# Layer 2 of a four-layer convolution kernel: PSUM tiles handed out in turn under names of their own

## The chip, the cores and the metric

One core of one Trainium2 chip runs one program. The metric is the device time of an execution in microseconds (us). Engines: PE is TensorE (its weight loads are listed as PEld), DVE is VectorE, ACT is ScalarE, POOL is GpSimd, SP is SyncE, which here issues the DMAs.

## The reference

An input of 32 images, 96 channels, 56 x 56, passes four layers, each of the form x = x + layer(groupnorm(x)), with 32 groups of three channels. Layer 0 is an inverted bottleneck with squeeze and excitation, layer 1 a wavelet convolution, layer 3 a depthwise 9 x 9 diffusion filter. The change is in layer 2, a quantised inverted bottleneck:

```python
h = bn(conv1x1(groupnorm(x), quant_w(w1)))      # 96 -> 576 channels
h = act_q(h)                                    # clip to 0..1, round to 4 bits
h = bn(depthwise3x3(h, quant_w(w2)))            # 576 channels
h = act_q(h)
h = bn(conv1x1(h, quant_w(w3)))                 # 576 -> 96
y = x_n + h                                     # x_n: the layer's normalised input
return x + y
```

## The kernel before

The layers run one after the other. Layer 2 (`layer2`, from 3620 to 5390 us of the profiled execution) goes over the 32 images. An image has 3136 positions, in eight row tiles of 392; the 576 channels are five blocks k = 0 to 4, the last with 64 channels. The work is cut into steps, written as a letter with indices in the string `L2_ORDER`, and `run_steps` plays this string once per pass n; a `-` after a step takes the image before n, a `+` the one after. PE, DVE and ACT execute exactly in the order in which the steps are recorded (`manual_schedule`), so one pass mixes three images:

- `e` (`expand`, L1107): for block k and quarter i of the image, four float32r matmuls (a high and a low part of the input, two row tiles) into one PSUM tile `ps`; then one eviction by `evict` into `u`, with scale, bias and rounding to int16. 20 of them per image.
- `m` (`activate`): DVE clips `u` into the padded bf16 image `apad`.
- `a` (`depthwise`, L1126): the 3 x 3 filter as matmuls of 64 x 64 diagonal matrices, four quadrants of the array at a time. For k < 4 and half h, 144 matmuls go into two PSUM tiles `psd`, for k = 4 72 in two steps with one tile each; 648 matmuls and 18 tiles per image. `evict` takes each tile to `a` or `a2c`. The eviction of half h, tile x of block k is called a{k}{h}{x} here.
- `n` (`activate2`): DVE clips it. `j` (`project`, L1163): ten matmuls into one tile `psj`, four times per image; `d` (`add`, L1170): DVE adds it to the image `xt`.
- `u`, `v` (L1045, L1053): tiny matmuls for the group norm, one PSUM tile each, read by DVE. `h` (`high`, L1079) on ACT and `l` (`low`, L1085) on DVE make the two parts of the next image's input. `s` and `o` take statistics (`channel_stats`); `o` also stores a finished pair of images and loads a later one (`store_images` L169, `fetch` L1016, by SP).

`evict` runs on ACT (L1097), but for four steps per image on DVE (L1095):

```python
L2_ON_DVE = {"e00", "e20", "a301", "a201"}
```

The depthwise steps of a pass come in this order, with what lies between them:

```python
a00 a10 o- a11 n1 a01 a20 h1+ a30 a21 l0+ a31 n0 a40 l1+ n2 l2+ a41 n3 n4
```

All PSUM tiles of layer 2 have the same shape, 128 x 2 x 512 float32 (two banks), and come from one pool of four under the tag "mm" (L1003). When a tile is asked for, the pool takes one of its four places; a tile that takes a place waits for the reads of the tile that had it before. An image takes 44 tiles: 18 `psd`, 20 `ps`, 4 `psj`, `pn` and `pv`. After the last pass `store_norm` (L95) takes one more.

Of the kernel before, what the change touches and what calls it, by code (L numbers as in the profile page):

```python
# [10 lines left out]
F32 = mybir.dt.float32  # L11
# [6 lines left out]
PSUM = bass.MemoryType.PSUM  # L18
# [73 lines left out]
    nc.vector.bn_aggr(mv, st.rearrange("c a b -> c (a b)"))  # L92


def store_norm(tc, S, pool, psum, mv, dram, bias, room=None):  # L95


    nc = tc.nc
    if room is None:
        room = pool.tile([C, 6 * B + 1], F32, tag="room", name="room", bufs=1)  # L100
    mc, d, dv, ve = (room[:C, i * B : (i + 1) * B] for i in range(4))
    row = room[:C, 4 * B : 6 * B + 1]
    rstd = row[:, 0:B]
    ps = psum.tile([128, 2, 512], F32, tag="mm", name="pn")
    nc.vector.tensor_copy(mc, mv[:, :, 0])
    nc.tensor.matmul(ps[:C, 0, :B], S.grp, mc, start=True, stop=True)
    nc.vector.tensor_tensor(d, mc, ps[:C, 0, :B], ALU.subtract)
    nc.vector.tensor_tensor(dv, d, d, ALU.mult)
    nc.vector.tensor_tensor(dv, dv, mv[:, :, 1], ALU.add)
    nc.vector.tensor_tensor(d, mc, d, ALU.subtract)  # L110
    nc.tensor.matmul(ps[:C, 1, :B], S.grp, dv, start=True, stop=True)
    nc.vector.tensor_scalar(ve, ps[:C, 1, :B], EPS_GN, None, ALU.add)
    nc.gpsimd.tensor_tensor(rstd, ve, S.mhalf[:C, :B], ALU.pow)
    nc.vector.scalar_tensor_tensor(row[:, B : 2 * B], d, -1.0, rstd, ALU.mult, ALU.mult)
    if bias is None:
        nc.vector.memset(row[:, 2 * B :], 0.0)
    else:
        nc.vector.tensor_copy(row[:, 2 * B :], bias)
    tc.keep_in_program_order(nc.sync.dma_start(dram, row))


def run_steps(step, image, order, done=""):

    for n in range(-2, B + 2):
        for s in order.split():
            b = n + s.count("+") - s.count("-")
            if 0 <= b < B and not (b == 0 and s.rstrip("+-") in done):
                step[s[0]](image(b), *map(int, s.rstrip("+-")[1:]))  # L130
# [53 lines left out]
def layer0(ctx, tc, S, x, w, y0, norm1, tables, aside):  # L184
# [363 lines left out]
    with tc.manual_schedule(engines=MANUAL):  # L548
        run_steps(step, image, L0_ORDER, FIRST)
    store_norm(tc, S, sm, psum, mv_all, norm1, S.bias1, hc.rearrange("p h w -> p (h w)"))  # L550


# [434 lines left out]
def layer2(ctx, tc, S, k2, y1, y2, norm3):  # L987
# [11 lines left out]
    pool = ctx.enter_context(tc.tile_pool(name="l2", bufs=1))  # L999
    sm = ctx.enter_context(tc.tile_pool(name="l2s", bufs=3))  # L1000
    up = ctx.enter_context(tc.tile_pool(name="l2u", bufs=3))
    ap = ctx.enter_context(tc.tile_pool(name="l2a", bufs=6))
    psum = ctx.enter_context(tc.tile_pool(name="l2p", bufs=4, space=PSUM))  # L1003
    CC, HALF, N9 = NBLK - 1, 64, 2 * NBLK - 1
    w1, w3, diag, s1, o1, s2, o2, s3, o3 = k2.constants

# [15 lines left out]

    apad = padded(cp, nc, NBLK, BF16, "apad")
    mv_all = cp.tile([C, B, 2], F32, tag="mv2", name="mv2")
    ims = {}

    def image(b):

# [5 lines left out]
    def small(name):  # L1034
        return sm.tile([C, 1], F32, tag=name, name=name)
# [5 lines left out]

    def group_mean(im):
        mean, var = im["mv"][:, 0:1], im["mv"][:, 1:2]
        ps = psum.tile([128, 2, 512], F32, tag="mm", name="pn")
        nc.tensor.matmul(ps[:C, 0, 0:1], S.grp, mean, start=True, stop=True)  # L1045
        gm, d, dv = (im.setdefault(n, small(n)) for n in ("gm", "d", "dv"))
        nc.vector.tensor_copy(gm, ps[:C, 0, 0:1])
        nc.vector.tensor_tensor(d, mean, gm, ALU.subtract)
        nc.vector.scalar_tensor_tensor(dv, d, d, var, ALU.mult, ALU.add)

    def group_variance(im):
        ps = psum.tile([128, 2, 512], F32, tag="mm", name="pv")
        nc.tensor.matmul(ps[:C, 0, 0:1], S.grp, im["dv"], start=True, stop=True)  # L1053
        ve = small("ve")
        nc.vector.tensor_scalar(ve, ps[:C, 0, 0:1], EPS_GN, None, ALU.add)
        im["rstd"] = small("rstd")
        nc.gpsimd.tensor_tensor(im["rstd"], ve, S.mhalf[:C, :1], ALU.pow)
# [34 lines left out]
    def evict(out, ps, s, o, c, on_dve):  # L1092

        if on_dve:
            nc.vector.tensor_scalar(out, ps, s[:, c : c + 1], o[:, c : c + 1], ALU.mult, ALU.add)  # L1095
        else:
            nc.scalar.activation(out, ps, AF.Identity, bias=o[:, c : c + 1], scale=s[:, c : c + 1])  # L1097

    def expand(im, k, i):

        if i == 0:
            im["u"][k] = up.tile([128, HW], I16, tag="u", name="u")
        ps = psum.tile([128, 2, 512], F32, tag="mm", name="ps")
        for j in range(2):
            r0 = (2 * i + j) * RT
            for part in ("hi", "lo"):
                nc.tensor.matmul(  # L1107
                    ps[:, j, :NT], w1[:, k * 128 : k * 128 + 128],
                    im[part][:, r0 : r0 + RT, :].rearrange("c h w -> c (h w)"),
                    start=(part == "hi"), stop=(part == "lo"),  # L1110
                )
        evict(im["u"][k][:, 2 * i * NT : 2 * (i + 1) * NT].rearrange("p (j n) -> p j n", j=2), ps[:, :, :NT],
              s1, o1, k if k < CC else N9 - 1, f"e{k}{i}" in L2_ON_DVE)
# [7 lines left out]
    def quarter(ps, k, t, r, c, j, tile):  # L1121

        p, q = (slice(x * HALF, (x + 1) * HALF) for x in (r, c))
        at = (tile * RT + t // 3) * PITCH + t % 3
        v = apad[k][p, at : at + RT * PITCH].rearrange("p (r w) -> p r w", w=PITCH)[:, :, 0:W]
        nc.tensor.matmul(ps[q, j, :NT].rearrange("p (r w) -> p r w", w=W), diag[p, k, t, :], v,  # L1126
                         start=(t == 0), stop=(t == 8))

    def depthwise(im, k, h):


        if h == 0:
            im["a2"][k] = (ap.tile([128, HW], BF16, tag="a2", name="a2") if k < CC else
                           ap.tile([128, HW // 2], BF16, tag="a2c", name="a2c", bufs=2))
        u = im["a2"][k].bitcast(I16)
        if k == CC:
            ps = psum.tile([128, 2, 512], F32, tag="mm", name="psd")
            for t in range(9):
                for c in range(2):
                    for j in range(2):  # L1140
                        quarter(ps, k, t, c ^ j, c, j, 4 * h + 2 * c + j)
            parts = [(h, ps, N9 - 1)]
        else:
            ps = [psum.tile([128, 2, 512], F32, tag="mm", name="psd") for _ in range(2)]
            for t in range(9):
                for j in range(2):
                    for x in range(2):
                        for r in range(2):
                            quarter(ps[x], k, t, r, r ^ x, j, 4 * h + 2 * x + j)
            parts = [(2 * h, ps[0], k), (2 * h + 1, ps[1], CC + k)]  # L1150
        for x, (n, p, c) in enumerate(parts):
            evict(u[:, 2 * n * NT : 2 * (n + 1) * NT].rearrange("p (m j x) -> p j m x", j=2, m=NPH),
                  p[:, :, :NT].rearrange("p j (x m) -> p j m x", m=NPH), s2, o2, c, f"a{k}{h}{x}" in L2_ON_DVE)
# [2 lines left out]
        clip(im["a2"][k], im["a2"][k].bitcast(I16))  # L1156

    def project(im, i):
        ps = im["ps"][i] = psum.tile([128, 2, 512], F32, tag="mm", name="psj")
        for j in range(2):  # L1160
            for k in range(NBLK):
                n, c = (2 * i + j, k + CC * (i % 2)) if k < CC else (2 * (i // 2) + j, N9 - 1 + i % 2)
                nc.tensor.matmul(ps[:C, j, :NT], w3[:, c, :], im["a2"][k][:, n * NT : (n + 1) * NT],  # L1163
                                 start=(k == 0), stop=(k == CC))
# [10 lines left out]
    def store(im):  # L1175
# [6 lines left out]

    step = {
        "s": stats, "u": group_mean, "v": group_variance, "b": residual_factors, "x": centre,
        "h": high, "l": low, "r": residual, "e": expand, "m": activate, "a": depthwise, "n": activate2,
        "j": project, "d": add, "o": store,
    }
    with tc.manual_schedule(engines=MANUAL):
        run_steps(step, image, L2_ORDER)
    store_norm(tc, S, sm, psum, mv_all, norm3, None)  # L1190


def diffusion_kernels(tc, cp, w, behind):
# [111 lines left out]
def kernel_body(tc, w, x, out):  # L1305
    nc = tc.nc
    with ExitStack() as ctx:
# [32 lines left out]
        with ExitStack() as ctx2:  # L1340
            k2 = Layer2(ctx2, tc, S, w, y1)

            def behind(pair):
                k2.prepare(pair)
                if not k2.stages:
                    k2.begin(min(2 * pair, C - GR))

            layer1(tc, w, y0, norm1, t1, t2, t3, y1, behind)
            k2.begin(C)
            layer2(tc, S, k2, y1, y2, norm3)  # L1350
# [143 lines left out]
```

## Time and profile before

| | |
|---|---|
| median of 3 runs | 5833.67 us (5833.61 to 5834.31) |
| profiled execution | 5845.79 us, span 5844.0 us |
| PE busy | 5504.4 us (94% of the span), 59688 matmuls |
| VectorE busy | 4693.6 us (80%) |
| ScalarE busy | 4182.6 us (72%) |
| depthwise matmuls of layer 2, L1126 | 935.9 us busy, 128.1 us idle before them |
| evictions of layer 2 on ScalarE, L1097 | 448 of `psd` to `a` (424.1 us), 576 of `ps` (536.9 us) |

A row of the page names line, engine, operation, and output<-inputs with shapes; then the number of instructions, their busy time and mean length in ns, and the idle time of the engine just before them with what ended it. "issue" stands for idle time that ended with no semaphore that the profile shows. A line of a timeline has start and length in us, engine, line, operation, how many were merged, and in brackets the idle time before it and its releaser. Times inside the span are counted from its start.

### The profile page before, as it was taken

The page shows a single profiled execution, that of the slowest core. Times are in us where ns is not written, and L with a number is a line of the kernel's source. Part 1 is how long each engine was busy: PE and PEld are TensorE (multiplying, and loading weights), DVE is VectorE, ACT ScalarE, POOL GpSimd, SP SyncE. Part 2 cuts the span into 40 slices and gives each one's busy share as a digit, 9 for nine tenths or more (in the row PEclk, how much of TensorE's full clock was granted, in tenths as well). Part 3 has the DMA queues.
Part 4 walks back from the last instruction along what each step waited for, and adds up shares of the span by engine and source line. Part 5 has one row for each costly group of instructions (what it writes and reads, how often), then busy time and mean ns, then how long its engine had stood idle before and what let it go on. Part 6 is the DMA issues. An engine that isn't in the chain of part 4 may idle for free.

```text
span 5844.0 us, 137224 instructions
## 1 busy us (share of the span) xinstructions
PE 5504.4 (94%) x59688; PEld 3074.4 (53%) x59688; DVE 4693.6 (80%) x5388; ACT 4182.6 (72%) x6036; POOL 240.1 (4%) x156
## 2 busy tenths in 40 slices
PE   5999999999999999995999997999899999897899
PEld 2333333333333333333566665777777777775444
DVE  6999999999999999994766665766667667665777
ACT  5888888888888888874565564766667677675555
POOL 5000000000000000000000000000000000000000
PEclk9999999999999999997999999999999999999999
DMA  3122333332222222235576668386796796754888
GB/s 98 18 56 56 62 60 57 58 58 54 56 49 48 55 52 56 46 26 89 144 141 147 154 147 89 26 44 42 49 46 37 51 49 40 50 31 34 234 253 245
DMA packets 1306412, 454.32 MB, mean 78 GB/s; under 512 B 1123841, under 2 KB 1301753, under 8 KB 1303889
## 3 DMA queue, kind: packets, MB, share of 16 engines
q1 hardware_dynamic: 1305809, 445.54, 50.3%
q8 instruction: 468, 7.67, 0.6%
q14 instruction: 135, 1.11, 0.1%
HBM read 284.44 MB, written 214.08 MB: 85 GB/s over the span
## 4 chain that ended last, share of the span: by engine, by line
PE 83%; ACT 6%; issue 4%; DVE 3%; DMA 2%; POOL 1%; SPq 1%; POOLq 0%; ACTq 0%; DVEq 0%
PE psd L432 17%; PE psd L1126 11%; PE psj L483 10%; PE ps L365 7%; PE pc L842 7%; PE ps L1107 7%; PE pse L388 6%; PE pc L1280 6%; PE psj L1163 3%; ACT hi L1079 2%; PE pc L826 2%; ACT a L1097 2%; PE pa L800 2%; PE pc L816 1%; ACT u L1097 1%
## 5 line engine op out<-in xcount | busy, mean ns | idle before, releaser
L406 DVE SCALAR_TENSOR_TENSOR h<-hpad,l_wdw,h 128x3136 f32<-128x3136 f32 x512 | 1782.2, 3481 | 9.1
L432 PE MATMUL psd<-plane,filt 128*32 128x392 f32 (+5 forms) x16384 | 1084.3, 485 | 0.0
L1126 PE MATMUL psd<-apad,diag 64*64 64x392 bf16 x20736 | 935.9, 333 | 128.1 <-issue 73.0
L1126 PEld LDWEIGHTS <-diag 64*64 64x64 bf16 x20736 | 705.0, 107 | 354.9 <-issue 184.8
L432 PEld LDWEIGHTS psd<-plane,filt 128*32 128x32 f32 (+1 forms) x16384 | 390.1, 108 | 675.2 <-issue 622.7
L1097 ACT ACTIVATE a<-psd,o,s 128x784 int16<-128x784 f32 x448 | 424.1, 999 | 347.8 <-PE psd L1126 347.7
L672 ACT COPY T<-raw 32x112 f32<-32x112 f32 (+2 forms) x1440 | 462.6, 384 | 267.6 <-DMA raw<-tdiff 219.9
L1097 ACT ACTIVATE u<-ps,o,s 128x784 int16<-128x784 f32 x576 | 536.9, 1003 | 160.2 <-PE ps L1107 141.8
L365 PE MATMUL ps<-xn,l_wboth 96*128 96x392 f32 (+1 forms) x1536 | 465.4, 505 | 23.9 <-ACT xn L347 23.0
L406 DVE SCALAR_TENSOR_TENSOR hc<-hhalf,l_wdw,hc 128x1568 f32<-128x1568 f32 x256 | 473.8, 1851 | 16.1 <-ACT hc L399 9.4
L1107 PE MATMUL ps<-hi,l_w1q 96*128 96x392 f32 x1280 | 461.7, 361 | 9.2 <-ACT hi L1079 9.2
L1280 PE MATMUL pc<-x,T 128*112 128x416 f32 (+1 forms) x1152 | 416.2, 524 | 40.3 <-DMA raw<-tdiff 39.6
L842 PE MATMUL pc<-x,T 128*112 128x416 f32 (+1 forms) x1152 | 445.9, 523 | 0.0
L1107 PE MATMUL ps<-lo,l_w1q 96*128 96x392 f32 x1280 | 437.3, 342 | 0.2 <-issue 0.2
L388 PE MATMUL pse<-xn,l_wboth 96*32 96x392 f32 x4096 | 391.2, 500 | 3.2 <-ACT hab L409 3.2
L365 PEld LDWEIGHTS ps<-xn,l_wboth 96*128 96x128 f32 (+1 forms) x1536 | 219.2, 173 | 248.8 <-issue 56.5
L1280 PEld LDWEIGHTS pc<-x,T 128*112 128x112 f32 x1152 | 204.8, 178 | 251.2 <-issue 233.3
L409 ACT ACTIVATE hab<-psd,o,s 128x784 f32<-128x784 f32 x256 | 284.1, 1114 | 58.6 <-PE psd L432 55.8
L375 ACT ACTIVATE hpad<-ps,o,s 128x784 f32<-128x784 f32 x256 | 278.4, 1104 | 49.2 <-PE ps L365 47.9
L483 PE MATMUL psj<-h,wg 128*32 128x392 f32 x3072 | 307.0, 514 | 1.4 <-DVE wg L472 1.4
L483 PE MATMUL psj<-hab,wg 128*32 128x392 f32 x3072 | 304.3, 510 | 0.0
L392 ACT ACTIVATE plane<-pse,o,s 128x784 f32<-128x784 f32 x256 | 256.2, 1001 | 24.9 <-PE pse L388 19.8
(234 smaller groups left out, 7608.2 us busy)
## 6 DMA issues: line engine op xcount, KB each, us to landing
X<-y SPq DMA_DIRECT2D x192, 392.0 KB
y<-xt SPq DMA_DIRECT2D x180, 392.0 KB
xt<-in_x_dram SPq DMA_DIRECT2D x16, 2352.0 KB
y<-y SPq DMA_DIRECT2D x96, 392.0 KB
xt<-y SPq DMA_DIRECT2D x96, 392.0 KB
out_dram<-y SPq DMA_DIRECT2D x96, 392.0 KB
twav<-zwav SPq DMA_DIRECT2D x768, 36.8 KB
raw<-twav SPq DMA_DIRECT2D x96, 168.0 KB
```

What stands on the lines that cost most here:

```text
L365: nc.tensor.matmul(ps[p, j, :NT], wexp[:, k * 128 : k * 128 + 128][:, m], im["xn"][:, j, rows, :].rearrange("c h w -> c (h w)"), start=Tru ...
L388: nc.tensor.matmul(ps[f * GC : (f + 1) * GC, half, :NT].rearrange("p (r w) -> p r w", w=W2), wexp[:, c : c + GC], im["xn"][:, f % 2, r0 : ...
L406: nc.vector.scalar_tensor_tensor(h2, taken(im, k, t), wdw[:, k, t : t + 1], h2, ALU.mult, ALU.add)
L409: nc.scalar.activation(view, ps, AF.Silu, bias=bi[1][:, c : c + 1], scale=sc[1][:, c : c + 1], accum_out=accum)
L432: nc.tensor.matmul(ps[at * GC : (at + 1) * GC, r, :NT].rearrange("p (r w) -> p r w", w=W2)[:, r0 - half * n : r1 - half * n, q0:q1], filt[ ...
L483: nc.tensor.matmul(ps[s * GC : (s + 1) * GC, t, :NT].rearrange("c (m r q) -> c r q m", m=2, q=W4), wg[p, k, c * GC : (c + 1) * GC], phases ...
L672: nc.scalar.copy(to.rearrange("x t (p s) -> x t p s", p=NPH), v[:, k])
L842: nc.tensor.matmul(ps[:PH, to], st["T"][j][:, h, k, :], st["x"][:, j, h, of], start=False, stop=(n == NK - 1))
L1097: nc.scalar.activation(out, ps, AF.Identity, bias=o[:, c : c + 1], scale=s[:, c : c + 1])
L1107: nc.tensor.matmul(ps[:, j, :NT], w1[:, k * 128 : k * 128 + 128], im[part][:, r0 : r0 + RT, :].rearrange("c h w -> c (h w)"), start=(part ...
L1126: nc.tensor.matmul(ps[q, j, :NT].rearrange("p (r w) -> p r w", w=W), diag[p, k, t, :], v, start=(t == 0), stop=(t == 8))
L1280: nc.tensor.matmul(ps[:, :, to], st["T"][:, h, k, :], st["x"][:, h, :, of], start=(n == 0), stop=(n == NK - 1))
```

## The change

Layer 2's pool gets one buffer per tag, and `bank` gives the tags mm1, mm2, mm3, mm0 in turn, in the order in which the steps are recorded. Every place in `layer2` that asked the pool for a tile now asks `bank`; `store_norm` gets the tag mm0. There are four tiles as before, and no step is moved.

```diff
--- before.py
+++ after.py
@@ -92,7 +92,7 @@
     nc.vector.bn_aggr(mv, st.rearrange("c a b -> c (a b)"))
 
 
-def store_norm(tc, S, pool, psum, mv, dram, bias, room=None):
+def store_norm(tc, S, pool, psum, mv, dram, bias, room=None, tag="mm"):
 
 
     nc = tc.nc
@@ -101,7 +101,7 @@
     mc, d, dv, ve = (room[:C, i * B : (i + 1) * B] for i in range(4))
     row = room[:C, 4 * B : 6 * B + 1]
     rstd = row[:, 0:B]
-    ps = psum.tile([128, 2, 512], F32, tag="mm", name="pn")
+    ps = psum.tile([128, 2, 512], F32, tag=tag, name="pn")
     nc.vector.tensor_copy(mc, mv[:, :, 0])
     nc.tensor.matmul(ps[:C, 0, :B], S.grp, mc, start=True, stop=True)
     nc.vector.tensor_tensor(d, mc, ps[:C, 0, :B], ALU.subtract)
@@ -1000,7 +1000,7 @@
     sm = ctx.enter_context(tc.tile_pool(name="l2s", bufs=3))
     up = ctx.enter_context(tc.tile_pool(name="l2u", bufs=3))
     ap = ctx.enter_context(tc.tile_pool(name="l2a", bufs=6))
-    psum = ctx.enter_context(tc.tile_pool(name="l2p", bufs=4, space=PSUM))
+    psum = ctx.enter_context(tc.tile_pool(name="l2p", bufs=1, space=PSUM))
     CC, HALF, N9 = NBLK - 1, 64, 2 * NBLK - 1
     w1, w3, diag, s1, o1, s2, o2, s3, o3 = k2.constants
 
@@ -1022,7 +1022,12 @@
 
     apad = padded(cp, nc, NBLK, BF16, "apad")
     mv_all = cp.tile([C, B, 2], F32, tag="mv2", name="mv2")
-    ims = {}
+    ims, turn = {}, [0]
+
+    def bank(name):
+
+        turn[0] += 1
+        return psum.tile([128, 2, 512], F32, tag=f"mm{turn[0] % 4}", name=name)
 
     def image(b):
 
@@ -1041,7 +1046,7 @@
 
     def group_mean(im):
         mean, var = im["mv"][:, 0:1], im["mv"][:, 1:2]
-        ps = psum.tile([128, 2, 512], F32, tag="mm", name="pn")
+        ps = bank(name="pn")
         nc.tensor.matmul(ps[:C, 0, 0:1], S.grp, mean, start=True, stop=True)
         gm, d, dv = (im.setdefault(n, small(n)) for n in ("gm", "d", "dv"))
         nc.vector.tensor_copy(gm, ps[:C, 0, 0:1])
@@ -1049,7 +1054,7 @@
         nc.vector.scalar_tensor_tensor(dv, d, d, var, ALU.mult, ALU.add)
 
     def group_variance(im):
-        ps = psum.tile([128, 2, 512], F32, tag="mm", name="pv")
+        ps = bank(name="pv")
         nc.tensor.matmul(ps[:C, 0, 0:1], S.grp, im["dv"], start=True, stop=True)
         ve = small("ve")
         nc.vector.tensor_scalar(ve, ps[:C, 0, 0:1], EPS_GN, None, ALU.add)
@@ -1100,7 +1105,7 @@
 
         if i == 0:
             im["u"][k] = up.tile([128, HW], I16, tag="u", name="u")
-        ps = psum.tile([128, 2, 512], F32, tag="mm", name="ps")
+        ps = bank(name="ps")
         for j in range(2):
             r0 = (2 * i + j) * RT
             for part in ("hi", "lo"):
@@ -1134,14 +1139,14 @@
                            ap.tile([128, HW // 2], BF16, tag="a2c", name="a2c", bufs=2))
         u = im["a2"][k].bitcast(I16)
         if k == CC:
-            ps = psum.tile([128, 2, 512], F32, tag="mm", name="psd")
+            ps = bank(name="psd")
             for t in range(9):
                 for c in range(2):
                     for j in range(2):
                         quarter(ps, k, t, c ^ j, c, j, 4 * h + 2 * c + j)
             parts = [(h, ps, N9 - 1)]
         else:
-            ps = [psum.tile([128, 2, 512], F32, tag="mm", name="psd") for _ in range(2)]
+            ps = [bank(name="psd") for _ in range(2)]
             for t in range(9):
                 for j in range(2):
                     for x in range(2):
@@ -1156,7 +1161,7 @@
         clip(im["a2"][k], im["a2"][k].bitcast(I16))
 
     def project(im, i):
-        ps = im["ps"][i] = psum.tile([128, 2, 512], F32, tag="mm", name="psj")
+        ps = im["ps"][i] = bank(name="psj")
         for j in range(2):
             for k in range(NBLK):
                 n, c = (2 * i + j, k + CC * (i % 2)) if k < CC else (2 * (i // 2) + j, N9 - 1 + i % 2)
@@ -1187,7 +1192,7 @@
     }
     with tc.manual_schedule(engines=MANUAL):
         run_steps(step, image, L2_ORDER)
-    store_norm(tc, S, sm, psum, mv_all, norm3, None)
+    store_norm(tc, S, sm, psum, mv_all, norm3, None, tag="mm0")
 
 
 def diffusion_kernels(tc, cp, w, behind):
```

## The prediction

> **What bounds the kernel now.** First the span in stretches: layer 2 runs from 3620 to 5390 us. In its middle (columns: start:end, length, busy us of PE, weight load, VectorE, ScalarE, GpSimd, granted clock, DMA share, GB/s):
> ```profile
> 4200.00:5400.00 1200.00, 1088.04 (x16620) 894.50 (x16613) 809.30 (x1349) 806.13 (x806) 16.33 (x21) 0.98 0.70 43
> ```
> TensorE (PE) is busy 91%, VectorE and ScalarE 67% each: PE sets the pace, so an idle microsecond of PE is one of the span. Then the waits of PE from 3620 to 5390 (us, times, longest), and the group's row on the page:
> ```profile
> PE psd L1126 <- issue: 73.0, 52, 4.4
> PE psd L1126 <- ACT a L1097: 52.1, 53, 1.8
> ...
> L1126 PE MATMUL psd<-apad,diag 64*64 64x392 bf16 x20736 | 935.9, 333 | 128.1 <-issue 73.0
> ```
> Nearly all idleness lies in the depthwise step, in two kinds. "ACT a" waits for an eviction that frees a PSUM tile. Numbering images 0 to 31 by their depthwise stretch, it falls in the same four places of images 4, 6, ... 28 and nowhere else but once. Image 20, in the order of time on PE, ScalarE and VectorE:
> ```profile
> 4751.69 6.99 PE L1126 MATMUL psd<-apad,diag 64*64 64x392 bf16 x150
> 4760.38 3.24 PE L1126 MATMUL psd<-apad,diag 64*64 64x392 bf16 x70 [1.70 <-ACT a L1097]
> 4764.57 0.36 PE L1126 MATMUL psd<-apad,diag 64*64 64x392 bf16 x2 [0.94 <-ACT a L1097]
> 4765.46 3.24 PE L1126 MATMUL psd<-apad,diag 64*64 64x392 bf16 x70 [0.54 <-ACT a L1097]
> 4769.65 2.56 PE L1126 MATMUL psd<-apad,diag 64*64 64x392 bf16 x56 [0.95 <-ACT a L1097]
> ...
> 4756.41 3.16 ACT L1079 ACTIVATE hi<-xt,rstd 96x784 fp32r<-96x784 f32 x2
> 4759.37 0.96 ACT L1097 ACTIVATE a<-psd,o,s 128x784 int16<-128x784 f32 x1
> ...
> 4755.55 1.09 DVE L1095 TENSOR_SCALAR a<-psd,s,o 128x784 int16<-128x784 f32 x1 [3.63 <-PE psd L1126]
> 4758.59 1.09 DVE L1095 TENSOR_SCALAR a<-psd,s,o 128x784 int16<-128x784 f32 x1 [1.95 <-PE psd L1126]
> ```
> The two VectorE evictions (steps a201, a301) end at 4756.6 and 4759.7. ScalarE's eviction of a300 stands behind 3.16 us of "hi" and ends at 4760.33, 0.05 us before PE goes on.
>
> The second kind, "issue", is no PSUM wait. Image 17, and image 29 that has none of either:
> ```profile
> 4589.76 5.62 PE L1126 MATMUL psd<-apad,diag 64*64 64x392 bf16 x128 [2.46 <-issue]
> 4597.35 6.88 PE L1126 MATMUL psd<-apad,diag 64*64 64x392 bf16 x152 [1.96 <-issue]
> ...
> 5234.59 28.08 PE L1126 MATMUL psd<-apad,diag 64*64 64x392 bf16 x648
> ...
> q8 instruction: 468, 7.67, 0.6%
> ```
> The stops lie 128 matmul and weight-load pairs apart: 256 instructions. PE's 119,968 recorded instructions over the 468 packets of the instruction queue are 256 each, so these are late instruction blocks. They go with SP's transfers, of which each pair of images has one store and one load:
> ```profile
> 4521.04 32.78 SPq L169 DMA_DIRECT2D y<-xt  x6
> 4553.98 37.56 SPq L1016 DMA_DIRECT2D xt<-y  x6
> ```
>
> **What the Trainium skill says.** "Perfetto Trace Analysis", Matmuls: independent matmul groups should rotate through different PSUM banks, so that one's evacuation overlaps the next one's matmuls. Image 29 rotates and has no wait; image 20 doesn't. "Runtime: NRT & Kernel Launch", Instruction fetch mechanics: instructions come in 16 KiB blocks of 256 by the sequencer's own DMA queue while the current block runs, the cost "mostly hidden". The size agrees; hidden it is not (73 us). "DMA: Bandwidth & Descriptors", Queues, rings and completion order: a DMA engine takes turns between its queues. The trace agrees in direction: a fetch packet takes 0.9 us beside a store, 2.2 us beside a load, and starts 2 to 6 us after its turn came.
>
> **The change, part by part.** In the built programs no instruction is added, removed or moved on any engine, and waits differ on PE alone; PE's count is the same, so its blocks begin at the same instructions.
>
> *Removed.* The built program before hands the 18 tiles of an image's depthwise step out as ABCD ABCD ABCD A CACAC in the 13 images 4, 6, ... 28 (A to D: tiles of two banks each), and as ABCD throughout in the other 19; after, ABCD in all 32. So in the 13 images a21's second tile no longer waits for a300's late ScalarE eviction, but for a201's on VectorE, over at 4756.6 in image 20 when PE needs it at 4758.7. a31's first tile waits for a300 (4760.33, needed a step of 3.1 us later, 4761.8), its second for a301 (4759.7), a40 and a41 for a21's two evictions (1.9 us after a21's end, needed 3.1 us after). No stop is left. Price: a matmul here starts every 28.08/648 = 0.043 us, while its modelled end is 0.33 us after its start, so each stop costs its idle time and 0.29 us more: 13 x 4 = 52 stops, 52.1 + 52 x 0.29 = 67 us (added up by starts in the 13 images: 67.1).
>
> *Given back in the same image.* Beside a store, the trace's fetch packets start at about 8.0, 14.4, 20.6 and 27 us after the store's start, whatever PE does; data take 0.93 us, and the block begins no sooner than some 1.45 us later: ready at 10.4, 16.8, 23.0, 29.4. A block without stops lasts 5.45 us, less than this grid of 6.3. The PSUM stops fall in the last two blocks and hide their fetches. Image 18 (store at 4630.16) enters its third block 16.6 us after; without stops it is through at 22.1 but gets the next at 23.0, and the one after at 29.4 in place of 28.5: 1.8 us back. So block by block: nine images some 1.8 us, images 8 to 14 (blocks falling later, or well before the grid) about 0.45: 9 x 1.8 + 4 x 0.45 = 18 us. Check: images 2 and 30 rotate already, with a store beside them, and take 31.51 and 32.59 us; the 13 take 35.1 on average, 3.1 x 13 = 40 us by this road, against 67 - 18 = 49.
>
> *Given back in the odd image.* It starts 3.7 us earlier against its load, whose time hangs on the store. Fetches there also come about every 6.3 us: 3.7 us more of PE in this stretch lose 3.7 x 0.85/6.3 = 0.5 us, 12 x 0.5 = 6 us. Single images will jump by a slot: from -2 us each (first fetch caught earlier) to +3, -24 to +36 us in all.
>
> *Moved.* In the pool's order the expand tile after the first projection waits for VectorE's eviction of e00; now the projection itself, 1.66 us earlier, does. Image 16:
> ```profile
> 4502.10 1.09 DVE L1095 TENSOR_SCALAR u<-ps,s,o 128x784 int16<-128x784 f32 x1
> ...
> 4503.41 0.83 PE L1163 MATMUL psj<-a,l_w3q 128*96 128x392 bf16 x4
> ```
> It ends 0.22 us before PE gets there (0.22 to 0.24 in 30 of 31 images, 0.71 in one). I take nothing; with a semaphore's way on top at most 0.3 x 31 = 9 us. Behind PE would be the expand tiles that feed ScalarE. Other tiles' waits move by a place or two among evictions that ended before.
>
> *Hidden elsewhere?* Between depthwise stretches PE is full (21 us: 80 matmuls at 0.178, 40 at 0.166). ScalarE and VectorE keep up with 49.5 us per image in images 1 and 29. A pair is loaded some 25 us before it is read, so 4 us less per two images is there to take. Layer 3 starts after layer 2's last store: the gain passes on whole.
>
> Sum: 67 - 18 - 6 = 43 us. The profiled execution took 5845.79 us (span 5844.0), 12 above the median of the runs, 5833.67; the saving is taken from each: 5803 there, 5791 by the median.
>
> **Rivals.** *A: the fetches give nothing back.* Odd images start nearer the load's beginning, catch an earlier slot each and regain what even ones lose: about 65 us, 5769. For it: 31.2 us (image 17) to 26.4 (image 13) after the load's start is one slot, a stall of 2 to 4 us turned away; against: images 2 and 30. *B: the fetch is the bound.* Every stop returns as an instruction stop: 5834. For it: the 6.3 us grid; against: only 4 or 5 blocks per image lie in the stretch, and layer 2's other 21 us per image give slack back. *C, slower: missed slots.* If each even image loses 1.8 us and each odd one misses a whole further slot, 6.3 us, 18 + 12 x 6.3 = 94 us go against 67: 27 us slower, 5861. It decides from (67 - 18)/12 = 4.1 us per odd image. A stop that long also halves the clock: the granted clock fell for 3.4 us after image 11's 4.69 us stop ("TensorE: Matmul & The Clock Gate", What's actually happening, gives about 3.4 us of idleness for that). Against: odd images lose 3.7 us in all now, in 1 to 3 stops. *D: the change is in name only,* as the same banks might have been chosen: excluded, 13 images differ in the built program.
>
> **Numbers.** Forecast (saving 20 to 58) 0.68, A 0.20, B 0.08, C 0.04. What a measurement of this kernel can tell from no change is 0.2%, 12 us. Faster by more takes the forecast, A and a little of B: 0.90; within 0.06; slower 0.04. Range: A's end with a fetch gain on top, 70 us, to 19 us, which leaves most of B and C out: 5764 to 5815.
>
> **What would show it.** Right: PE's waits on "ACT a" at L1126 gone but for one or two; depthwise stretches of the 13 images at 29 to 33 us; "issue" stops grown from 73 to 85 to 110 us; the projection without a wait on VectorE. Wrong: "ACT a" waits elsewhere, a wait "DVE u" before psj of 0.3 us or more, "issue" unchanged (A) or above 130 us (B, C).

## The result, and the profile after

The changed kernel takes 5761.34 us (median of 4 runs, 5759.47 to 5772.8) against 5833.64: 0.9883 of before, 95% interval 0.9865 to 0.9900, a saving of 72 us by the medians and 68 by the ratio, which goes by means. The forecast was 43 us, 5791, with a range down to 5764; the time lies at its lower edge (5761 by the median, 5765 by the ratio), where rival A stood (5769).

The profiled execution took 5772.8 us (span 5771.0). The middle of layer 2, before and then after. The prediction's window ran to 5400 us and so took in the end of layer 2, where PE has little to do; this one doesn't:
```profile
4200.00:5300.00 1100.00, 1015.33 (x15466) 840.41 (x15463) 761.88 (x1271) 762.64 (x762) 10.89 (x20) 0.99 0.71 44
4200.00:5300.00 1100.00, 1056.40 (x16269) 868.36 (x16262) 792.33 (x1317) 795.01 (x796) 10.94 (x20) 1.00 0.73 45
```
PE is busy 96%, where it was 92%, and its granted clock is 1.00, not 0.99. PE's waits in layer 2, and the group's row on the page (the change moves L1126 to L1131):
```profile
PE psd L1131 <- issue: 64.6, 68, 3.6
PE psd L1131 <- ACT a L1102: 1.3, 1, 1.3
...
L1131 PE MATMUL psd<-apad,diag 64*64 64x392 bf16 x20736 | 913.2, 329 | 68.3 <-issue 64.6
```
The waits for ScalarE's evictions are gone, but for the one outside the 13 images. The "issue" stops are more in number, 68 for 52, and less in sum. Image 20, an even one, and image 17, an odd one, on PE's timeline:
```profile
4684.51 15.54 PE L1131 MATMUL psd<-apad,diag 64*64 64x392 bf16 x353
4700.74 5.62 PE L1131 MATMUL psd<-apad,diag 64*64 64x392 bf16 x128 [0.70 <-issue]
4706.95 5.63 PE L1131 MATMUL psd<-apad,diag 64*64 64x392 bf16 x128 [0.59 <-issue]
4713.44 1.88 PE L1131 MATMUL psd<-apad,diag 64*64 64x392 bf16 x39 [0.86 <-issue]
...
4530.97 16.24 PE L1131 MATMUL psd<-apad,diag 64*64 64x392 bf16 x369
4548.06 12.05 PE L1131 MATMUL psd<-apad,diag 64*64 64x392 bf16 x279 [0.85 <-issue]
```
An image's 648 matmuls are eight steps of 72 and two of 36 (a half of a block has 72, not the 144 given with the kernel). The PSUM stops of image 20 had stood at matmuls 434, 504, 506 and 576. It has none any more; instead it stops for instructions at matmuls 353, 481 and 609, and the fetches for the last two are those that the PSUM stops had hidden. Image 17 stops once, for 0.85 us, where it had stopped for 2.46 and 1.96.

The mean length of the depthwise stretches, from first matmul start to last end, tells where the time between these two executions came from:

| | before | after | saved |
|---|---|---|---|
| 13 images 4, 6, ... 28 | 35.12 us | 31.61 us | 13 x 3.51 = 45.7 us |
| 12 images 5, 7, ... 27 | 32.78 us | 30.26 us | 12 x 2.52 = 30.2 us |
| the 7 others | 30.58 us | 29.65 us | 6.5 us |

Between the stretches nothing changed (664.0 and 663.5 us in all). Of these 82 us the span shows 73: this execution entered layer 2 later by 8 us, after instructions that are the same in both.

### The profile page after: what moved, and what is told of

Same layout as the page of the kernel before. It is cut to its first block, busy times and chain, and to the rows that moved or that the text cites. A ratio compares the mean times of both kernels' runs of the same rounds, so it can differ in the third digit from the quotient of the medians.

```text
span 5771.0 us, 137224 instructions
## 1 busy us (share of the span) xinstructions
PE 5488.4 (95%) x59688; PEld 3064.9 (53%) x59688; DVE 4689.3 (81%) x5388; ACT 4184.5 (73%) x6036; POOL 239.8 (4%) x156
## 4 chain that ended last, share of the span: by engine, by line
PE 82%; DMA 5%; ACT 4%; issue 3%; DVE 3%; SPq 1%; POOL 1%; POOLq 0%; ACTq 0%; DVEq 0%
PE psd L432 17%; PE psd L1131 12%; PE psj L483 11%; PE ps L365 7%; PE pc L842 7%; PE ps L1112 6%; PE pse L388 6%; PE pc L1285 4%; PE psj L1168 3%; PE pc L826 2%; ACT hi L1084 2%; PE pa L800 2%; DMA xt<-y 1%; PE pc L816 1%; DMA X<-y 1%
## 5 line engine op out<-in xcount | busy, mean ns | idle before, releaser
L1131 PE MATMUL psd<-apad,diag 64*64 64x392 bf16 x20736 | 913.2, 329 | 68.3 <-issue 64.6
L1131 PEld LDWEIGHTS <-diag 64*64 64x64 bf16 x20736 | 686.4, 106 | 291.1 <-issue 114.7
```

## The experiments

Lengths below are means over the same 13 even and 12 odd images of each run's profile. A time is compared by its ratio to the runs of before on the same chip.

**The order alone.** Four tags, but each tile gets the place that the pool had chosen:
```diff
-        return psum.tile([128, 2, 512], F32, tag=f"mm{turn[0] % 4}", name=name)
+        return psum.tile([128, 2, 512], F32, tag=f"mm{POOL_ORDER[turn[0] - 1]}", name=name)
```


> Four tags as in the changed kernel, but each tile gets the tag of the place that the pool chose before (a string of 1408 digits). Theory (the order of the places counts, not the names): the four ScalarE stops per image in images 4, 6, ... 28 are back, 52 stops and about 52 us in the waits view, and the time is that of before, 5834 us within 0.2%. Rival (separate tags, with one buffer each, are what helps, whatever the order): 5761 us, as the changed kernel.

Measured: 5818.44 us, 1.0000 of before (0.9989 to 1.0011). Its waits:
```profile
PE psd L1148 <- ACT a L1119: 54.2, 54, 1.8
PE psd L1148 <- issue: 46.2, 39, 3.4
```
The order of the places is the change; the names do nothing. One thing was not expected: the twelve executions spread from 5800 to 5830 us, and those of before on this chip from 5804 to 5835. This profile, of an execution at the lower end, has odd stretches of 30.95 us, not 32.78, and even ones of 34.45. What the fetches cost differs between executions of one order; the PSUM stops hardly do (52.1 and 54.2 us). So the 30 us of the odd images and the 6.5 of the others in the table above hang on the two executions that were profiled.

**The changed kernel again,** on a later chip.

> The changed kernel once more, on the chip of the three that follow, since executions of the old order spread over 5800 to 5834 us in the last comparison. Theory (52 PSUM stops, 67 us, go; the fetches take back 18 us in even images and, depending on where an odd image falls against its load, take or give some 0 to 30 us): 45 to 75 us under before, depthwise stretches of even images at 31.6 us, of odd images 29 to 31 us. Rival (the first comparison was a lucky pairing): under 40 us of saving, odd stretches no shorter than before's.

Measured: 5748.48 us, 0.9880 (0.9855 to 0.9906), 73 us under that chip's before; even stretches 31.09, odd ones 29.86 us. The first comparison was no luck.

**The loads left out,** with both orders. These kernels load no later pairs in layer 2 and go through the three pairs at hand again and again; the stores stay:
```diff
-            if b >= 2 * len(k2.pairs):
+            if len(k2.pairs) * 2 <= b < 6:
```


> The changed kernel without layer 2's loads of later pairs (L1016 inside the loop): it computes again and again on the three pairs loaded first, stores stay. Theory (odd images stop for instruction blocks only because of the load): their stretches fall from 30.3 to 28.1 us and those of even images stay at 31.6 us, beside a store; 12 x 2.2 = 26 us less, about 5735 us. Rival (other traffic or the order of steps makes them stop): odd stretches stay near 30 us.

> The pool's old order of places by tags, again without the loads of later pairs. Theory (what the change brings beyond 67 - 18 us comes from the odd images' place against the load): without loads the two orders differ by the even images alone, 13 x 3.5 = 46 us, and odd stretches are 28.1 us in both; about 5781 us. Rival (the new order helps odd images in itself, or nothing is given back in even ones): 67 us or more between the two.

Measured: in turn 5728.45 us (0.9838, 0.9819 to 0.9858), in the pool's order 5770.23 us (0.9910, 0.9894 to 0.9926): 42 us apart, give or take some 15. In turn, then in the pool's order:
```profile
PE psd L1131 <- issue: 42.0, 40, 3.0
```
```profile
PE psd L1148 <- ACT a L1119: 51.7, 53, 1.8
PE psd L1148 <- issue: 24.3, 26, 2.4
```
Odd stretches are 28.08 and 28.07 us, those of a depthwise step that never stops; even ones are 31.51 and 34.75. So without loads the orders differ in the even images alone, 13 x 3.24 = 42 us. The 52 PSUM stops went, and 18 us of "issue" stops came in their place, 42.0 for 24.3. With the loads the difference is 73 us: the other 31 us, give or take some 20, need the load. That they lie in the odd images follows from the stretches, since those are alike without loads and the even ones differ by nearly as much as with them (42 and 46 us).

**PE held up between an even image and the odd one after it,** in the changed kernel:
```diff
-        for j in range(2):
+        for j in range(2) if i or im["b"] not in range(4, 29, 2) else (0, 1, 0, 1, 0, 1):
```


> The changed kernel with PE held up by 20 more matmuls (the first projection of images 4, 6, ... 28 computed three times over, 3.3 us each image, 43 us in all) between the depthwise stretch of an even image and that of the odd one after it; no PSUM stop is added. Theory (an odd image's fetches miss a place when it starts some 3.5 us later against its load): odd stretches grow from 30.3 us back to 32 or 33, and the time rises by 43 and another 25 to 30 us, to about 5832 us. Rival (the odd images' gain came from something else in the new order): odd stretches stay at 30.3 us and the time is 5761 + 43 = 5804 us.

Measured: 5825.43 us, 1.0009 (0.9998 to 1.0020). Against the changed kernel's 0.9883 that is 73 us more. The matmuls added were priced at 43 of them; in the profile PE's time between the stretches grew by 49, since three of the 13 projections took 1.5 to 2.9 us longer than the others. Its waits:
```profile
PE psd L1131 <- issue: 82.9, 58, 4.3
PE psd L1131 <- ACT a L1102: 3.6, 3, 2.2
```
Odd stretches went from 30.26 to 32.63 us, 12 x 2.37 = 28 us, with no PSUM stop added in them (the two that came, 2.2 and 1.1 us, are in images 22 and 26); even ones stayed at 31.50. A delay of the odd image is enough to make it slower, whatever the cause.

**Halved and quartered DMAs.** Layer 2's stores and loads of y are cut along their rows (for the loads; the stores likewise):
```diff
 for to, of in groups(pair, y1, lambda y: y[:, :, b : b + 2, :]):
-    nc.sync.dma_start(to, of)
+    for r in range(0, H * NPH, H * NPH // 2):
+        nc.sync.dma_start(to[:, r : r + H * NPH // 2], of[:, r : r + H * NPH // 2])
```


> The changed kernel with layer 2's stores and loads of y each issued as two DMAs of half the size (12 per pair in place of 6, same bytes). Theory (PE's instruction blocks are fetched only where SP's next DMA begins, about every 6.3 us, and a block lasts 5.45 us): places for a fetch come every 3.2 us, nearly all 'issue' stops of L1131 go, 65 us to under 20 us in the waits view, and the time falls by 50 to 80 us from 5761 to about 5695 us. Rival (the fetch is slow because the DMA engines share their bandwidth with the transfers, whatever their size): stops and time as in the changed kernel, 5761 us.

> The pool's old order of places by tags, with the halved DMAs. Theory (two independent kinds of stops, which share time only through the fetches): with the fetches out of the way the 52 PSUM stops cost their full 67 us and nothing else, so this kernel lies 67 us (60 to 72) over the one in turn with halved DMAs, about 5762 us, and the depthwise stretches of odd images are alike in both. Rival (the odd images' gain has to do with the PSUM order itself): 72 us or more between them, and odd stretches longer here than there.

Measured: in turn 5696.70 us (0.9791, 0.9777 to 0.9806), in the pool's order 5749.85 us (0.9881, 0.9867 to 0.9896). In turn, then in the pool's order:
```profile
PE psd L1133 <- issue: 12.5, 21, 2.7
```
```profile
PE psd L1150 <- ACT a L1121: 56.5, 54, 2.2
PE psd L1150 <- issue: 13.1, 16, 1.4
```
The same bytes in half-size pieces: the "issue" stops fall from 64.6 to 12.5 us and the time by 54 us, give or take 13 (from a ratio of 0.9883 to 0.9791), inside the 50 to 80 forecast. Packets (nearly all under 512 bytes) and rate did not change: from 3650 to 5200 us the DMA engines move 44 GB/s in the changed kernel, 46 with halves and 46 with quarters. So it is not shared bandwidth, the rival, that made PE wait. Even stretches are 28.26 and 33.18 us, odd ones 29.54 and 29.69, alike. By the profiles the orders lie 66 us apart from layer 2's first depthwise matmul to its last, by the times 53, give or take 12. The profile in the pool's order is of the slowest of four executions and the one in turn of the fastest, so the times count for more, and 67 us lies just outside them.

> The changed kernel with each of layer 2's stores and loads of y issued as four DMAs (24 per pair). Theory (a fetch waits for the next DMA's beginning): with a place every 1.6 us the stops left with halves, 12.5 us in the waits view, go as well: about 5685 us, 5 to 12 us under the halves. Rival (more issues cost DMA time, or SP falls behind and loads come late): 5697 us or more, with a wait of VectorE on xt<-y.

> The kernel in turn with quartered DMAs once more, as the reference for its neighbours on this chip: 5682 us, 2.4% under before.

> The pool's old order of places by tags, with layer 2's stores and loads of y as four DMAs each. Theory (with the fetches out of the way nothing is given back and nothing gained beside): 67 us over the kernel in turn with quartered DMAs, 60 to 70 by the times, with four stops in each of images 4, 6, ... 28 of 2.05, 1.28, 0.89 and 1.28 us from matmul to matmul. Rival (halved DMAs gave 53 us by the times because a PSUM stop is cheaper without the profiler): 50 to 56 us.

> The kernel in turn with stores and loads of y as eight DMAs each (48 per pair). Theory (the 5 us of stops left with quarters are the last of the fetch waits): 5677 to 5682 us, no clear gain. Rival (SP's issue time[...] or smaller DMAs slow the transfers until a load comes late): over 5690 us.

Measured: quarters in turn 5682.07 us (0.9760, 0.9741 to 0.9778) and again 5686.83 us (0.9774); in the pool's order, beside the latter, 5745.36 us (0.9873, 0.9857 to 0.9890), 58 us more; eighths in turn 5681.58 us (0.9764, 0.9749 to 0.9779). Quarters in turn are 10 and 18 us under halves by the ratios, forecast 5 to 12. "Issue" stops were 5.0, 5.7, 1.0 and 0.8 us. With quarters, even stretches are 28.07 us in turn and 33.17 in the pool's order, 13 x 5.10 = 66 us apart; odd ones are longer by 0.55 us in turn, 7 us, which leaves 60. So the forecast of 67 was right for the stops in the profile, while the whole difference is 60 us there and 58 by the times, between the theory's 60 to 70 and the rival's 50 to 56. That stops are cheaper without the profiler is not needed to explain it, nor excluded. Eighths bring nothing clear beyond quarters and cost nothing, with 0.49 us in the median for SP to issue one. Quarters in turn beat both kernels: 2.3% under before, 1.1% under the change.

**Why a300's eviction was late.** The pool's order with quarters, "hi" moved:
```diff
-    e41 e23 b+ e42 j3- x+ e32 e33 m2 d3- m3 s++ e43 h0+ m4 a00 a10 o- a11 n1 a01 a20 h1+ a30 a21 l0+
+    e41 e23 b+ e42 j3- x+ e32 e33 m2 d3- m3 s++ e43 h0+ m4 a00 a10 o- a11 n1 a01 h1+ a20 a30 a21 l0+
```


> The pool's order with quartered DMAs, and the step h1+ (ScalarE's two 'hi' instructions) moved from behind a20 to before it, so that a300's eviction no longer stands behind 3.2 us of 'hi'. Theory (the first stop is that eviction's lateness, the other three are those of two places in turn): the first stop falls from 2.05 to about 1.27 us, the others stay, 13 x 0.78 = 10 us less than with h1+ in its place. Rival (the first stop is like the others, from the two places alone): 2.05 us as before.

Measured: 5733.07 us, 0.9854 (0.9840 to 0.9869), 12 us under the same with h1+ in its place. An even image on PE:
```profile
4685.91 3.24 PE L1150 MATMUL psd<-apad,diag 64*64 64x392 bf16 x70 [0.93 <-ACT a L1121]
4690.10 0.36 PE L1150 MATMUL psd<-apad,diag 64*64 64x392 bf16 x2 [0.95 <-ACT a L1121]
4690.99 3.24 PE L1150 MATMUL psd<-apad,diag 64*64 64x392 bf16 x70 [0.54 <-ACT a L1121]
4695.18 3.23 PE L1150 MATMUL psd<-apad,diag 64*64 64x392 bf16 x72 [0.94 <-ACT a L1121]
```
The first stop fell from 1.72 us of idleness (mean of the 13 images with quarters) to 0.93, from matmul to matmul 2.05 to 1.26; the other three stayed. Those come from two places in turn, the first one's excess from "hi".

## Why the prediction was right or wrong

**The PSUM stops: right.** All four places of the 13 images are clear after; forced back by tags they return with the time of before; with the fetches out of the way they cost 64 to 66 us in the profiles, forecast 67, and the two orders lie 53 to 58 us apart by the times.

**What even images give back: right in kind, somewhat short in size.** Forecast 18 us, and a stretch of 29 to 33 us. The means went from 35.12 to 31.61 us, 46 us saved where 49 and, by the road of images 2 and 30, 40 had been worked out; without loads 42 were. Against 67 us of stops that is 21 to 25 us given back. The idle time alone grew by 18 us without loads (42.0 for 24.3), but an instruction stop too costs more than its idle time.

**What odd images give back: wrong, and it made the miss.** The step "3.7 us more of PE in this stretch lose 0.5 us, 12 x 0.5 = 6 us" stands in the forecast where odd images gained time, 30 us in the first two profiles. The text did allow for up to 24 us of gain, "first fetch caught earlier", and put it at a net loss. It took the odd image's place against the load's fetch grid as spread evenly, so that hits and misses would cancel. They don't, since every odd image follows an even one in step with the same store. In the trace of before, ten of the 12 odd images entered the first block of their stretch 26 to 28 us after the load's start and had its successor fetched at 30 to 33. After the change they begin earlier against the load; image 17, 22.5 us after the load's start before, begins 19.1 us after this one:
```profile
4511.88 36.62 SPq L1016 DMA_DIRECT2D xt<-y  x6
```
Now eleven of the 12 enter at 23 to 25 us and are fetched at 25 to 27. One whole place is gained in nearly every pair, not a share of one; the second profile of each order (places forced by tags, changed kernel again) shows the same two groups. The run with PE held up undoes it. That is rival A's mechanism, to which the text gave 0.20; its note named the slot at 26.4 us in image 13, and images of before at 26 to 27 us were the evidence that it lay just out of reach. How much this is worth is less sure than that it is there: with two profiles of each order it is 8 us by the nearest (30.95 to 30.26), 35 by those furthest (32.78 to 29.86), 22 by their means, and 31 by the times with and without loads.

**The clock: left out of the sum.** In layer 2 before, the granted clock falls to half for 3.4 us ten times, nine of them in odd images; after, once. In the second profiles it is four times and never. The same length of image 23's stretch before, first at half clock and then at full:
```profile
4913.20:4916.50 3.30, 3.30 (x44) 2.32 (x47) 0.47 (x1) 1.90 (x2) 0.00 (x0) 0.50 1.56 60
4918.00:4921.30 3.30, 3.30 (x88) 2.73 (x80) 0.00 (x0) 1.90 (x2) 0.00 (x0) 1.00 1.72 56
```
PE does 44 matmuls in place of 88. Worked out from the starts of the 361 matmuls that run at half clock in odd images, this cost 12.8 us before and nothing after. The idle time before odd images' matmuls went from 38.8 to 21.3 us. So of the 30 us some 13 were the clock and 17 the stops. The prediction named the half clock only under rival C, for long stops like image 11's, and the length of idleness that it quotes there was not needed: the stops ahead of these ten windows were idle for 1.97 to 4.37 us. Nor was such a stop always enough: one of 2.46 us brought no half clock.

**The moved wait on VectorE: right.** e00's eviction ends and the projection starts, in the changed kernel:
```profile
4664.66 1.09 DVE L1100 TENSOR_SCALAR u<-ps,s,o 128x784 int16<-128x784 f32 x1
```
```profile
4666.00 0.83 PE L1168 MATMUL psj<-a,l_w3q 128*96 128x392 bf16 x4
```
0.25 us remain, 0.21 to 0.25 in all 31 images, and PE's waits name no VectorE here.

**The rivals, and one sign that failed.** "Issue" stops were to grow to 85 to 110 us by the forecast and to over 130 by B and C; they fell to 64.6. So B and C are out, and the forecast's own sign failed with its odd images: these lost 19 us of such stops, while even ones got 15 more. D is out, as the old order under new names takes the time of before.

## What to carry to other kernels

A pool that picks a free buffer can settle into using two of four; look for one stop that repeats in the same places of every other iteration, and see which buffers the tiles there were given. When a stop is taken away, list what else became due inside it (here instruction blocks), and ask what starts earlier after it: in a loop that runs in step with its transfers a shift doesn't average out but hits or misses a place in every iteration. Small DMAs can be worth more than large ones while an engine with a dense instruction stream is the bound.

## What the runs showed of the hardware

A fetch of PE's next 16 KiB instruction block didn't merely get slower beside SP's transfers. In odd images without loads its packet started 0.2 us before the current block's first matmul, on average. Beside transfers of 392 KB it began, in the median, 1.0 to 1.2 us after SP had begun to issue a next DMA (traces of after and before); these beginnings lie 6.3 us apart, so starts spread evenly would have a median of some 3 us. With halves the median was 1.2 us at a spacing of 3.1, which by itself shows little. From a block's first matmul to the start of the next block's fetch it took 2.4 us before and 2.6 after, as a mean over the blocks of all stretches, 1.4 with halves and 0.7 with quarters. With a block lasting 5.45 us that decides whether PE waits: 73, 65, 12 and 5 us of stops. That the fetch packet queues behind the descriptors already handed out is the likely reason; no run looked into the queue.
